# A graph layer and a routed expert layer on one core: when result rows are summed, how fast slot work is issued, batches of 6, 5 and 3, and 28 row buffers

## The chip, the cores and the metric

The kernel runs on one core of a Trainium2 chip. The metric is the device time of one execution in microseconds (us), as a median over several executions; beside it stands one profiled execution, whose trace gives the durations of single instructions. A core has five engines with their own instruction queues: PE (matmuls; PEld is its weight load), DVE (vector), ACT (scalar), POOL and SP. Each queue runs in the order in which the program issued its instructions. An instruction that waits holds up all that stand behind it on its engine. Here SP issues the plain transfers, and POOL the gathers, which fetch 128 rows by an index list.

## The reference

There are 6250 nodes of 256 features and 100,000 edges, sorted by target. First a graph layer, then a layer of 8 experts of which each node uses two:

```python
h = layernorm(x)
agg = segment_sum(h[src], dst) / maximum(degree, 1)
x = x + concatenate([h, agg], 1) @ W.T + b
t = layernorm(x)
xn = layernorm(t) * gamma + beta
w = softmax over the two largest of (xn @ Wr + br)
y = sum over those two experts e of w[e] * (gelu(xn @ W1[e] + b1[e]) @ W2[e] + b2[e])
out = x + y
```

## The kernel before

A prologue (to about 70 us) normalizes x and multiplies it by the neighbour half of W; the result goes to DRAM as `z_d`, so that the edges gather rows that are already multiplied. The own half follows as `u_d`, in pieces beside the first edges.

The edges are cut into 56 windows (`W`) of 14 tiles (`C`) of 128 edges: 784 edge tiles, counted by `t`. Per tile, POOL gathers 128 rows of `z_d` into one of `XG` buffers `xg` in a ring (`gather`, L553), and PE adds them into the window's 128 target rows by a matmul with a one-hot matrix `hot` (`add_edges`, L570), which DVE builds for seven tiles at a time (`hot_tiles`, L564). The gather issued in step `t` is that of tile `t + XG`. When a window is full, its first row is joined with the row that it shares with the window before (`shared_row` L576, by way of `keep_sums`, `put_sums`, `share_row` and SP), then divided by the degree and added to the own part (`window_x1`, L605 to L607; `load_u` fetches that part, for the last window by a POOL gather, L599), and stored as `x1_d`.

Four windows (`CW`) make a group, 14 in all. After a group's last window its nodes are normalized and routed, then sorted by expert into slots: PE sorts (L652), ACT copies runs of nodes to their slots `xe` (`copy_runs`, L786). Then comes the slot work on 128 slots for each expert: `hidden` (16 matmul instructions L811 and Gelu on ACT, L816) and `result` (8 matmul instructions L824, and DVE adds the bias and empties the single PSUM buffer `py`, L828), after which SP writes the rows to the batch's `y`. Nodes that don't fit in an expert's 128 slots go to extra tiles of the batch (`more_stages`, L854 to L879). `BATCHES` gives for each batch the number of groups and of extra tiles; a batch's rows of `y` may be gathered only when all its slot work is issued (`B.left == 0`). If the extra tiles do not suffice, a flag is set and a slow branch at the end computes everything anew.

At the end each window's result is summed: `gather_rows` loads `x1_d` through SP and gathers two rows of `y` per node on POOL (L913), `add_rows` adds them with their weights on DVE (L920, two instructions) and `store` writes the output through SP (L898), the last window through POOL (L900). That makes 112 row gathers for 56 windows.

All engines' order is written out by the program at build time. `at(t, f)` puts the routing steps of a group at fixed steps after its last window (`Steps`; `LastSteps` for the last group). `after(t)` is called after each edge tile and then on: it runs what is due, then takes slot work from the queue `tasks` as far as `pace` allows. Each piece has an assumed cost: 2.0 for half a pair of `hidden`, 1.75 for `result`, 1.7, 0.5 and 1.75 for an extra tile, so 30 for a group (8 and 8 pieces) and 3.95 for an extra tile. The pace in the edge loop is `rate`, set when a group's slot work starts (54 steps after its last window, 25 for the last group), such that each piece of work is done by its deadline; afterwards it is 2.0. `sum_rows` is called last in each step; it works with an assumed `clock`, and keeps gathers and adds apart:

```python
clock += 0.6 if t < W * C else 0.3 if tasks else 1.2
...
    spent -= us
    clock += us
```

Row sums begin when fewer than 100 tiles are left. Those that begin while edge tiles are still to be gathered use tiles of their own, `o` and `y2`; the later ones use the ring `xg` (`spare`).

Of the kernel before, what the change touches and what calls it, by code (L numbers as in the profile page):

```python
# [8 lines left out]
F32 = mybir.dt.float32  # L9
# [8 lines left out]
P = 128  # L18
EPS = 1e-5
C = 14  # L20
TB = 4
UB = 2
CW = 4
CAP = 64
BATCHES = (6, 7), (6, 5), (2, 3)
GB = 3
XG = 24


@with_exitstack  # L30
def gnn_ffn_kernel(ctx: ExitStack, tc: tile.TileContext, x, x_cols, src, dst, dst_next, gw, gw_t, gb, gb_cols, gamma, beta,
# [33 lines left out]
    N, D = x.shape  # L65
    NX, H = w1.shape[0], w1.shape[2]
# [18 lines left out]
    batches = []  # L85
    for n, tiles in BATCHES:
        B = Group()
        B.first, B.n, B.tiles = sum(b.n for b in batches), n, tiles
        B.at = HS + XS * sum(b.tiles for b in batches)
        B.more_row = n * NX * SH  # L90
        B.rows = B.more_row + XS * tiles
        B.left, B.deadline = n * NX * SH // (2 * P) + tiles, None
        batches.append(B)

    const = ctx.enter_context(tc.tile_pool(name="const", bufs=1))
# [373 lines left out]

    xg = [edges.tile([P, DA], F32, name=f"xg{i}") for i in range(XG)]  # L470
    for g in xg:
# [432 lines left out]

    def gather_rows(K, j, V):
        g = K.first + j
        gathered = now >= W * C - XG
        V.o = spare() if gathered else slots.tile([P, D], F32, name="o", bufs=2)
        nc.sync.dma_start(V.o, x1_d[g * P:(g + 1) * P, :])
        G, i = K.group, j  # L910
        V.y2 = [spare() if gathered else slots.tile([P, D], F32, name="y2", bufs=4) for _ in range(2)]
        for r in range(2):
            nc.gpsimd.indirect_dma_start(  # L913
                out=V.y2[r], out_offset=None, in_=K.batch.y[:, :],
                in_offset=bass.IndirectOffsetOnAxis(ap=G.rows[:, r, i:i + 1], axis=0))

    def add_rows(K, j, V):
        G, i = K.group, j
        for r in range(2):
            nc.vector.scalar_tensor_tensor(V.o, V.y2[r], G.w2[:, r, i:i + 1], V.o, op0=ALU.mult, op1=ALU.add)  # L920
        store(K, j, V.o)
# [1 line left out]

    tasks, later, Ks, sums, adds = [], {}, [], [], []
    slots, w1_sb, w2_sb, xe = None, None, None, None
    now, spent, rate, clock, due, spares = None, 0.0, 0.0, 0.0, 0.0, 0
    class Steps:  # L930

        x1, var, roots, norms, route, exps, weigh, choices, count = 2, 5, 7, 9, 11, 14, 15, 16, 19
# [1 line left out]
        runs, rest, place, tiles, copied, rows, pace, start = 30, 33, 36, 39, 40, 46, 1.5, 54  # L934

    class LastSteps:
# [3 lines left out]
        runs, rest, place, tiles, copied, rows, pace, start = 15, 16, 19, 24, 21, 28, 1, 25  # L940
# [37 lines left out]
        at(t + S.start, start_experts, K)  # L978

    def start_experts(K):  # L980
        nonlocal rate
        B = K.batch
        K.deadline = now + CW * C
        tasks.extend(expert_stages(K))
        if K.index == B.first + B.n - 1:
            B.deadline = now + 2 * CW * C
            tasks.extend(more_stages(B))
        Ks.append(K)
        rate, total = 0.0, 0.0
        for us, _, of in tasks:  # L990
            total += us
            rate = max(rate, 1.01 * total / max(1, of.deadline - now))
        rate = min(rate, 0.72)
        sums.extend((K, j) for j in range(CW))

    def sum_rows():

        nonlocal due
        while adds and (adds[0][0] <= clock or not (sums or tasks)):
            adds.pop(0)[1]()  # L1000
        left = W * C - 1 - now
        while sums and not sums[0][0].batch.left and clock >= due and left < 100:
            if 0 < left < XG and spares + 3 > XG - left:
                return
            K, j = sums.pop(0)
            V = Group()
            gather_rows(K, j, V)
            adds.append((clock + 8.0, lambda K=K, j=j, V=V: add_rows(K, j, V)))
            while len(adds) > XG // 3 - 1:
                adds.pop(0)[1]()  # L1010
            due = clock + 12.0 if left >= XG else max(due, clock - 6.0) + (4.0 if left > 0 else 2.4)

    def after(t):
        nonlocal now, spent, clock
        now = t
        while later.get(t):
            later[t].pop(0)()
        later.pop(t, None)
        clock += 0.6 if t < W * C else 0.3 if tasks else 1.2
        pace = rate if t < W * C else 2.0  # L1020
        spent = min(spent + pace, pace) if tasks else 0.0
        while tasks and spent > 0:
            us, f, _ = tasks.pop(0)
            spent -= us
            clock += us
            f()
        sum_rows()
# [7 lines left out]
    V = new_window(0, None)  # L1035
# [5 lines left out]
    for index in range(W // CW):  # L1041
        K = Group()
# [9 lines left out]
        for g in range(K.first, K.first + CW):  # L1052
            if g > 0:
                V = V_next
            for c in range(C):
                t = g * C + c
# [26 lines left out]
    t = W * C  # L1083
# [11 lines left out]
    with tc.If(wrong_r > 0), tc.tile_pool(name="gp", bufs=1) as gp:  # L1095
# [9 lines left out]
        with tc.For_i(0, W * C) as j:  # L1105
# [19 lines left out]
            spare = gp.tile([P, 1], F32, name="spare")  # L1125
# [110 lines left out]
```

## Time and profile before

| | |
|---|---|
| median of 3 executions | 1246.62 us (1244.07 to 1251.12) |
| profiled execution, own time | 1242.94 us |
| profiled execution, span from first to last instruction | 1240.9 us |
| busy: PE, PEld, DVE | 1039.6 (84%), 855.7 (69%), 704.7 (57%) us |
| busy: ACT, POOL | 457.3 (37%), 857.6 (69%) us |
| mean granted clock of PE | 0.944 |
| edge gathers | 784, of 0.95 us each, 70.3 to 1071.9 us |
| row gathers into `o`, `y2` | 14, 961.7 to 1060.6 us |
| row gathers into the ring | 98, 1073.1 to 1229.4 us |

A line of a group reads: source line, engine, operation, output <- inputs, count | busy time, mean ns of one | idle time of the engine just before, and what ended most of it. A line of the waits reads: engine, what waited <- for what: us in total, number of times, longest. A line of the timeline begins with start and duration in us. A busy POOL means that it writes a gather's descriptors; the rows land later (3.0 us after the start at the median of the edge gathers).

### The profile page before, as it was taken

The numbers are of one execution on the slowest core, as the hardware profiler recorded it, in microseconds if no ns is written. First come the engines' busy times: TensorE is split into PE (matmuls) and PEld (weight loads), VectorE is DVE, ScalarE is ACT, GpSimd is POOL, SyncE is SP. The second block draws the span as 40 slices with busy tenths as digits, with TensorE's granted clock in tenths as the row PEclk, the third lists the DMA queues.
The fourth block names the chain that finished last, engine by engine and source line by source line (L and its number), as shares of the span: only waits on it lengthen the run. The fifth ranks groups of instructions, "written<-read, shape, count | busy, mean of one in ns | idle before, by whom it ended". The sixth has DMA issues, their size and how long they took to land. (4 is left out here: it accounts for less than half of the span.)

```text
span 1240.9 us, 18842 instructions
## 1 busy us (share of the span) xinstructions
PE 1039.6 (84%) x5236; PEld 855.7 (69%) x5236; DVE 704.7 (57%) x2432; ACT 457.3 (37%) x1265; POOL 857.6 (69%) x907
## 2 busy tenths in 40 slices
PE   7997857699989888998989999998985787889770
PEld 6775645688867677776767988786764676758650
DVE  5765667475646465654547455564643644668442
ACT  2400002645453444353434536344342242535410
POOL 0057777777777777777777777777777777776615
PEclk9999987899999999999999999999998787999895
DMA  9989896455555545555555555555554555666644
GB/s 325 362 258 292 262 351 193 134 153 153 151 151 148 153 134 147 154 149 137 151 152 148 147 162 151 148 154 142 151 147 135 152 162 150 176 207 206 201 142 133
DMA packets 139188, 221.03 MB, mean 178 GB/s; under 512 B 23108, under 2 KB 106255, under 8 KB 138950
## 3 DMA queue, kind: packets, MB, share of 16 engines
q0 software_dynamic: 43104, 120.94, 37.4%
q1 hardware_dynamic: 87638, 89.37, 21.6%
q10 hardware_dynamic: 8336, 9.45, 2.3%
q8 instruction: 44, 0.72, 0.3%
q14 instruction: 66, 0.54, 0.1%
HBM read 166.69 MB, written 53.02 MB: 177 GB/s over the span
## 5 line engine op out<-in xcount | busy, mean ns | idle before, releaser
L553 POOL DMA_INDIRECT xg<-z_d,src_i x784 | 746.5, 952 | 307.0 <-issue 110.9
L570 PE MATMUL pS<-xg,hot 128*128 128x265 f32 x1568 | 440.2, 405 | 68.5 <-DMA xg<-z_d,src_i 50.2
L570 PEld LDWEIGHTS pS<-xg,hot 128*128 128x128 f32 x1568 | 287.3, 196 | 161.9 <-DMA xg<-z_d,src_i 86.5
L811 PE MATMUL ph<-xe,w_sb 128*128 128x128 f32 x1792 | 228.6, 283 | 21.5 <-ACT xe L786 20.7
L811 PEld LDWEIGHTS ph<-xe,w_sb 128*128 128x128 f32 x1792 | 224.9, 199 | 30.0 <-ACT xe L786 22.8
L824 PE MATMUL py<-w_sb,hid 128*128 128x256 f32 x896 | 214.9, 385 | 1.8 <-DVE rows L828 0.9
L816 ACT ACTIVATE hid<-ph,b_sb 128x128 f32<-128x128 f32 x448 | 127.4, 368 | 208.8 <-PE ph L811 208.6
L824 PEld LDWEIGHTS py<-w_sb,hid 128*128 128x128 f32 x896 | 171.0, 193 | 27.9 <-issue 2.0
L786 ACT ACTIVATE xe<-xs x448 | 139.4, 311 | 67.9 <-ACT xe L786 36.5
L564 DVE TENSOR_TENSOR hot<-cols,rel 128x896 f32<-128x896 f32 x112 | 121.1, 1081 | 72.5 <-PE pS L570 69.8
L913 POOL DMA_INDIRECT xg<-y_d,rows_i x98 | 94.7, 966 | 61.6 <-DMA y_d<-rows 25.6
L576 DVE TENSOR_TENSOR pS<-pS,row 1x265 f32<-1x265 f32 x55 | 23.5, 428 | 157.7 <-PE pS L570 146.8
L655 ACT ACTIVATE xs<-pm,beta_sb,gamma_sb 128x256 f32<-128x256 f32 x112 | 57.1, 561 | 129.3 <-PE pm L652 129.1
L580 ACT ACTIVATE sums<-pS 128x265 f32<-128x265 f32 x56 | 21.7, 388 | 178.1 <-DVE pS L576 76.5
L652 PE MATMUL pm<-to,xn 128*128 128x256 f32 x224 | 59.7, 390 | 21.6 <-DVE to L645 21.6
L255 PE MATMUL ph<-gc,x_t 128*128 128x264 f32 (+1 forms) x200 | 58.9, 420 | 15.4 <-DVE u_t L372 13.1
L920 DVE SCALAR_TENSOR_TENSOR xg<-xg,w,xg 128x256 f32<-128x256 f32 x98 | 46.5, 482 | 37.8 <-DMA xg<-y_d,rows_i 21.2
L828 DVE TENSOR_TENSOR rows<-py,b_sb 128x512 f32<-128x512 f32 x56 | 38.3, 685 | 51.9 <-PE py L824 51.7
L652 PEld LDWEIGHTS pm<-to,xn 128*128 128x128 f32 x224 | 43.2, 195 | 29.3 <-DVE to L645 21.7
L255 PEld LDWEIGHTS ph<-gc,x_t 128*128 128x128 f32 x200 | 38.7, 202 | 28.3 <-issue 13.0
L816 ACT ACT_TABLE_LOAD x24 | 30.8, 1283 | 67.4 <-PE ph L811 67.2
L255 PE MATMUL pm<-gc,x_t 128*128 128x264 f32 (+1 forms) x192 | 54.0, 406 | 0.0
(191 smaller groups left out, 840.2 us busy)
## 6 DMA issues: line engine op xcount, KB each, us to landing
y_d<-rows SPq DMA_DIRECT2D x56, 256.0 KB
xg<-z_d,src_i POOLq DMA_INDIRECT x784, 3.0
w_sb<-w_dram ACTq DMA_DIRECT2D x16, 512.0 KB
sums_d<-sums SPq DMA_DIRECT2D x55, 132.5 KB
x<-u_d SPq DMA_DIRECT2D x55, 132.0 KB
x_d<-x SPq DMA_DIRECT2D x56, 128.0 KB
u_d<-u_t SPq DMA_DIRECT2D x24, 264.0 KB
xg<-x_d SPq DMA_DIRECT2D x49, 128.0 KB
```

Source lines behind the costliest of these rows:

```text
L255: nc.tensor.matmul(pz, x_t[:, t, k, :], gc[:, h * KD + k, :n], start=(k == 0), stop=(k == KD - 1))
L553: nc.gpsimd.indirect_dma_start(out=xg[(g * C + c) % XG][:, :DZ], out_offset=None, in_=z_d[:, :], in_offset=bass.IndirectOffsetOnAxis(ap=sr ...
L564: nc.vector.tensor_tensor(hot, col[:, None, :].to_broadcast([P, HC, P]), V.rel[:, c:c + HC, None].to_broadcast([P, HC, P]), op=ALU.is_equal)
L570: nc.tensor.matmul(V.pS, V.hot[c // HC][:, c % HC, :], xg[(V.g * C + c) % XG], start=(c == 0), stop=(c == C - 1))
L652: nc.tensor.matmul(px[:, k, :], G.xn[i][:, k * P:(k + 1) * P], G.one_hot[i], start=True, stop=True)
L655: nc.scalar.activation(xs[:, at:at + 2 * P], px[:, k, :], AF.Identity, bias=beta_sb[:, k:k + 1], scale=gamma_sb[:, k:k + 1])
L786: nc.scalar.activation(xe[:, :, bass.ds(to_at, CAP)], src[:, :, bass.ds(src_at, CAP)], AF.Copy)
L811: nc.tensor.matmul(ph[:, i, a * SH:(a + 1) * SH], w1_sb[:, U.e + a, k, c * P:(c + 1) * P], xe[:, k, at:at + SH], start=(k == 0), stop=(k = ...
L816: nc.scalar.activation(U.hid[:, c, a * SH:(a + 1) * SH], ph[:, i, a * SH:(a + 1) * SH], AF.Gelu, bias=b1_sb[:, U.e + a, c:c + 1])
L824: nc.tensor.matmul(U.py[:, h, :], U.hid[:, c, h * P:(h + 1) * P], w2_sb[:, U.e + h, c, :], start=(c == 0), stop=(c == KH - 1))
L913: nc.gpsimd.indirect_dma_start(out=V.y2[r], out_offset=None, in_=K.batch.y[:, :], in_offset=bass.IndirectOffsetOnAxis(ap=G.rows[:, r, i:i ...
L920: nc.vector.scalar_tensor_tensor(V.o, V.y2[r], G.w2[:, r, i:i + 1], V.o, op0=ALU.mult, op1=ALU.add)
```

## The change

The second batch has five groups instead of six, the third three groups instead of two; the extra tiles stay at 7, 5 and 3. The ring has 28 buffers instead of 24, and so edge gathers are issued 28 tiles ahead. Row sums begin when fewer than `XG` = 28 tiles are left, which is after the last edge gather is issued, and they use the ring alone; `o` and `y2` are gone. The add of a window is put 10 instead of 8 on the assumed clock after its gathers, and eight instead of seven adds may be open. The deadlines go: the pace of slot work is 0.72 in the edge loop, 1.2 after it until the last group's slot work starts, then 2.0.

```diff
-BATCHES = (6, 7), (6, 5), (2, 3)
+BATCHES = (6, 7), (5, 5), (3, 3)
 GB = 3
-XG = 24
+XG = 28
...
     def gather_rows(K, j, V):
         g = K.first + j
-        gathered = now >= W * C - XG
-        V.o = spare() if gathered else slots.tile([P, D], F32, name="o", bufs=2)
+        V.o = spare()
         nc.sync.dma_start(V.o, x1_d[g * P:(g + 1) * P, :])
         G, i = K.group, j
-        V.y2 = [spare() if gathered else slots.tile([P, D], F32, name="y2", bufs=4) for _ in range(2)]
+        V.y2 = [spare() for _ in range(2)]
...
     def start_experts(K):
-        nonlocal rate
         B = K.batch
-        K.deadline = now + CW * C
         tasks.extend(expert_stages(K))
         if K.index == B.first + B.n - 1:
-            B.deadline = now + 2 * CW * C
             tasks.extend(more_stages(B))
         Ks.append(K)
-        rate, total = 0.0, 0.0
-        for us, _, of in tasks:
-            total += us
-            rate = max(rate, 1.01 * total / max(1, of.deadline - now))
-        rate = min(rate, 0.72)
         sums.extend((K, j) for j in range(CW))
...
         left = W * C - 1 - now
-        while sums and not sums[0][0].batch.left and clock >= due and left < 100:
+        while sums and not sums[0][0].batch.left and clock >= due and left < XG:
             if 0 < left < XG and spares + 3 > XG - left:
                 return
             K, j = sums.pop(0)
             V = Group()
             gather_rows(K, j, V)
-            adds.append((clock + 8.0, lambda K=K, j=j, V=V: add_rows(K, j, V)))
+            adds.append((clock + 10.0, lambda K=K, j=j, V=V: add_rows(K, j, V)))
             while len(adds) > XG // 3 - 1:
                 adds.pop(0)[1]()
-            due = clock + 12.0 if left >= XG else max(due, clock - 6.0) + (4.0 if left > 0 else 2.4)
+            due = max(due, clock - 6.0) + (4.0 if left > 0 else 2.4)
...
         clock += 0.6 if t < W * C else 0.3 if tasks else 1.2
-        pace = rate if t < W * C else 2.0
+        pace = 0.72 if t < W * C else 1.2 if len(Ks) < W // CW else 2.0
```

More of the change, by code (lines that the diff above doesn't have):

```diff
@@ L91, in gnn_ffn_kernel @@
         B.rows = B.more_row + XS * tiles
-        B.left, B.deadline = n * NX * SH // (2 * P) + tiles, None
+        B.left = n * NX * SH // (2 * P) + tiles
         batches.append(B)
@@ L928, in gnn_ffn_kernel @@
     slots, w1_sb, w2_sb, xe = None, None, None, None
-    now, spent, rate, clock, due, spares = None, 0.0, 0.0, 0.0, 0.0, 0
+    now, spent, clock, due, spares = None, 0.0, 0.0, 0.0, 0
     class Steps:
```

## The prediction

> **What bounds the kernel now.** The chain that ended last holds two pieces only (the final scatter), so I read the other views: the costliest groups first, then busy time in stretches of 50 us, the waits, and the timeline of the last 300 us.
>
> ```profile
> L553 POOL DMA_INDIRECT xg<-z_d,src_i x784 | 746.5, 952 | 307.0 <-issue 110.9
> L913 POOL DMA_INDIRECT xg<-y_d,rows_i x98 | 94.7, 966 | 61.6 <-DMA y_d<-rows 25.6
> ```
>
> The 784 edge gathers take 952 ns each, with 0.30 us between two. The first starts at 70.3, tile 672 at 915.3: one per 1.257 us. Counting the rows of L570 beside those of L553, PE consumes tile 196 to tile 672 only 2 to 5 us behind POOL, about what a gather needs to land (3.0 us median). So through the middle **POOL sets the pace** and PE follows. Then, by stretch (PE, PEld, DVE, ACT, POOL, clock, DMA share, GB/s):
>
> ```profile
> 650.00:700.00 50.00, 50.00 (x257) 41.19 (x256) 36.00 (x129) 23.91 (x68) 37.82 (x40) 1.00 0.55 147
> 700.00:750.00 50.00, 49.64 (x288) 43.71 (x287) 28.75 (x90) 23.38 (x63) 37.93 (x40) 1.00 0.56 155
> ...
> 950.00:1000.00 50.00, 31.96 (x148) 27.15 (x147) 22.16 (x76) 14.39 (x42) 37.81 (x41) 0.80 0.51 140
> 1000.00:1050.00 50.00, 35.73 (x183) 31.23 (x181) 24.08 (x81) 15.46 (x40) 37.81 (x41) 0.83 0.57 158
> ...
> 1200.00:1250.00 50.00, 6.61 (x33) 5.06 (x31) 9.71 (x20) 2.28 (x8) 16.27 (x17) 0.67 0.32 95
> ```
>
> From 950 to 1050 PE loses 18.0 + 14.3 = 32 us while POOL goes on. The waits name it, and a second hole:
>
> ```profile
> DVE o L920 <- DMA y<-y_d,rows_i: 48.9, 11, 21.0
> POOL xg L913 <- DMA y_d<-rows: 25.6, 1, 25.6
> ```
>
> The first: an early add of result rows stands in DVE's queue for a gather that POOL reaches only after the edge gathers issued ahead of it. DVE sits from 943.5 to 964.5:
>
> ```profile
> 943.31 0.17 DVE L640 TENSOR_SCALAR q<-q 128x8 f32<-128x8 f32 x1
> 964.48 0.48 DVE L920 SCALAR_TENSOR_TENSOR o<-y,w,o 128x256 f32<-128x256 f32 x1 [20.99 <-DMA y<-y_d,rows_i]
> ```
>
> After it PE is some 20 us behind POOL and stays there: the last edge gather starts at 1071.9, its matmul at 1092.3.
>
> ```profile
> 1071.88 0.95 POOL L553 DMA_INDIRECT xg<-z_d,src_i  x1 [0.30 <-PE pS L570]
> 1092.33 0.61 PE L570 MATMUL pS<-xg,hot 128*128 128x265 f32 x2
> ```
>
> The second hole is the end: POOL is out of rows it may gather at 1185 and waits for the last batch's y.
>
> ```profile
> 1207.43 0.43 DVE L876 TENSOR_TENSOR rows<-py,b_sb 128x256 f32<-128x256 f32 x1 [2.15 <-PE py L872]
> 1210.55 0.94 POOL L913 DMA_INDIRECT xg<-y_d,rows_i  x1 [25.57 <-DMA y_d<-rows]
> 1229.42 0.95 POOL L913 DMA_INDIRECT xg<-y_d,rows_i  x1 [0.30 <-issue]
> 1233.73 1.02 POOL L900 DMA_INDIRECT out_dram<-xg,tail_i  x1 [3.36 <-DVEq L1095]
> ```
>
> So the end is: last y evacuated (Y = 1207.9), 2.7 us until POOL gathers it, 16 gathers with 15 steps of 1.25, and 11.5 us from the start of the last gather to the end at 1240.9.
>
> **What the skill says.** "Perfetto Trace Analysis", DMA Instruction — SWDGE (GPSIMD): the profiled end of a gather is the end of descriptor writing, not of the move. The trace agrees: 0.95 us on POOL, 3.0 us to landing. The same page, What "DMA-bound" means: a kernel can be bound by the issuing engine's descriptor work; POOL's unbroken 37.8 of 50 us with the DMA engines at 0.55 is that. "TensorE: Matmul & The Clock Gate", HAM oscillation: idle gaps over about 3.4 us cost PE its clock; in the two stretches with the holes the granted clock is 0.80 and 0.83, else 1.00 around them.
>
> **The change by parts.** I count the loop by hand through its own quantities (tile t, queue of tasks, clock).
>
> *Sums behind the last edge gather.* With `left < 100` seven windows (gathers at t = 684, 695, 706 ...) put 14 row gathers among the edge gathers; with `left < 28` the first stands at t = 758, behind the last edge gather (t = 755). POOL drops 14 x 1.25 = 17.5 us ahead of the last edge gather: 1071.9 - 17.5 = 1054.4 (70.3 + 783 x 1.257 = 1054.5 agrees). The 14 gathers, 7 loads of x1 and 7 stores on SP are not removed but come later; all 112 row gathers now run after 1054, against 98.
>
> The wait on DVE is moved, not gone. Add 0 goes to t = 766. DVE arrives when tile 766 is consumed: 70.3 + 766 x 1.257 + 4 = 1037. Its second row gather starts at 1057 and lands 3.2 us later (median of L913): 1060.5. **A stall of 23 us**, like the 21.0 of before. Queued behind it on DVE: evacuations L828 (py has one buffer, so PE stops at the next result), hot tiles of window 55 (L564, t = 770), and L576, L605 to L607 of windows 54 and 55; on SP the store, then put_sums and share_row of window 54. From there add j can run at 1060.5 + 2.5 j. The last window's L605 (t = 785) stands behind add 6 (t = 784): 1075.5 + 1 = 1076.5. POOL's own queue is later still: the last window's x1 gather L599 (t = 782) stands behind 16 row gathers, 1055.7 + 16 x 1.25 = 1075.7, and lands 3.2 later, 1079; so L607 runs at 1079 where it ran at 1096.3 (L599 was behind 12 of them, at 1088.6, and not late). **17 us earlier**: what POOL saves, with the same lag as before. The stalls from 943 on go, but only this net counts.
>
> *Slot work at 0.72.* A group is 8 hidden (2.0) and 8 result (1.75), 30 us; an extra tile 3.95. The trace's durations fit: 16 matmuls of L811 in 1.95, 8 of L824 in 1.89. Before, group 11 starts at t = 725 with 30 + 19.75 for batch 1's five tiles, at rate 1.01 x 30 / 56 = 0.541; at 784 there are left 16.3 of tiles and 30 of group 12, 46.3 us, all done before group 13 starts (t = 808). After, batch 1 ends with group 10, its tiles run by t = 735, group 11 is done by 777, and group 12 has 26 us left at 784, which 1.2 a step takes in the 24 steps. **20 us less** PE work between the last window and group 13. Before, that stretch took 1096.3 to 1151.4 (first L811 of group 13), 55 us with PE at 43 of 50, so less work shortens it; 35 remain. Does DVE allow that? Adds 7 to 20 stand in it: 14 x 2.5 = 35. Just.
>
> Does 0.72 overfill PE earlier? Before ran at 0.72 too, for t = 445 to 613 (about 635 to 845 us): PE was full there, its lag at most 7 us, POOL undisturbed. Cost nothing; the cover is the ring and the 14 of 56 steps that a group then leaves free. Without it POOL would lose the 7 us once per group at most.
>
> *28 buffers.* 35 us of ring for 30. POOL never stood for a full ring in the edge stage, so no gain; four more memsets, and 4.2 KB per partition against 6 KB of o and y2 given up: nothing. Unknown cost of a changed layout: I take 0, ends -1 and +3 (the page's 0.3 us idle before a gather, some ten times). Delay 10 for 8 and eight open adds for seven give the rows more time: in with the stalls.
>
> *Batches 6, 5, 3.* 15 extra tiles as before, but after the last y there are 24 gathers, not 16: **8 x 1.25 = 10 us more at the end**.
>
> Sum on the profiled span: Y = 1207.9 - 17 - 20 = 1171; end = 1240.9 - 37 + 10 = **1214**. Check by POOL: 88 gathers from 1055.7 at 1.25 end at 1166, at before's own 1.367 (81 steps in 1073.1 to 1183.9) at 1176. The last 24 then start between 1171 + 2.7 and 1176, giving 1214 to 1216. I take 1214. The profiled execution took 1242.94, 2.0 over its span; the median 1246.62 is 3.7 above that. So 1214 + 5.7 is **1220**. Floor: 897 gathers (784, 112 and L599), 896 steps of 1.25 from 70.3 with no hole, and the same 11.5: 1202, so 1208.
>
> **Rivals.** (1) *The stall eats the rest.* The last group's routing is chained to adds that POOL paces, so only the 17.5 us reach Y: 1240.9 - 17.5 + 10 + 5.7 = 1239. For it: the 35 against 35 above. Against it: in 1075 to 1210 DVE waited only 4.0 us for row gathers. (2) *Slower: the ring of rows becomes the bound.* An add also needs the x1 load, and SP takes loads and stores in order; DVE waited 14.9 us for x1, up to 3.0 each. If each window cost 1.0 of adds and 3.0 of waiting, a gather takes 2.0 us: 1055.7 + 111 x 2.0 + 11.5 + 5.7 = 1295. It decides from 1.61 us a gather (slower by 0.5%), 1.56 for no gain; before showed 1.367 with seven open adds. (3) *It doesn't do what it says*: a fixed 0.72 leaves the last groups as they were, and only the 10 us more and the 17.5 less remain (as rival 1), or 5 or 3 extra tiles don't hold the batches' tokens and the slow branch runs; counted from the inputs they need 5 and 2, so that is out.
>
> **How the numbers follow.** A measurement of this kernel can tell about 0.5% (6.2 us) from no change. Forecast 0.75, rival 1 0.14, rival 2 0.06, rest 0.05. Rival 1 lies at the edge of faster and same: half to each. Faster 0.86, same 0.08, slower 0.06. Range: the floor less one for the layout, 1207, to rival 1 with one more, 1240.
>
> **What would show it.** Right: last L553 at about 1054; no L913 before it; a DVE wait on y_d gathers of 20 us or more at about 1037; PE over 40 of 50 us in 950 to 1000; Y near 1171; POOL's wait for y_d under 8 us; 24 gathers after it. Wrong: POOL slower than 1.26 us in the edge stage; row gathers over 1.5 us apart; Y after 1185.

## The result and the profile after

The changed kernel takes 1242.74 us at the median of 10 executions (1239.93 to 1244.05); the kernel before, run again beside it, 1246.68 (1243.91 to 1251.12). The ratio is 0.9967, with a 95% interval of 0.9953 to 0.9981: faster by a third of a per cent, where 2% were forecast. The profiled execution takes 1243.91 us, its span 1242.0. In three of the five batches of runs below every kernel, the one before among them, took 17 to 18% longer (before: 1453 to 1468 us), which is called the slower condition.

The groups of the kernel after, from its page:

```profile
L553 POOL DMA_INDIRECT xg<-z_d,src_i x784 | 747.7, 954 | 306.3 <-issue 115.5
L912 POOL DMA_INDIRECT xg<-y_d,rows_i x112 | 108.5, 969 | 61.4 <-issue 19.8
```

All 112 row gathers are now one group, and an edge gather costs what it did. The stretches (PE, PEld, DVE, ACT, POOL, clock, DMA share, GB/s):

```profile
950.00:1000.00 50.00, 50.00 (x233) 39.35 (x233) 30.77 (x106) 20.87 (x66) 37.81 (x41) 1.00 0.56 154
1000.00:1050.00 50.00, 49.75 (x294) 44.69 (x293) 31.73 (x117) 23.45 (x63) 37.81 (x41) 1.00 0.56 157
1050.00:1100.00 50.00, 31.55 (x176) 27.73 (x175) 26.38 (x84) 19.48 (x56) 36.82 (x38) 0.83 0.63 185
```

The hole of 950 to 1050 is filled: PE 50.00 and 49.75 where it had 31.96 and 35.73. A new one opens behind the last edge gather, and the granted clock falls to 0.83 there, as the Trainium skill, "TensorE: Matmul & The Clock Gate", HAM oscillation, would have it (PE stands idle for 12.3 us at one point). The timeline of the kernel after around the last edge gather, DVE's part and POOL's:

```profile
1059.43 0.48 DVE L919 SCALAR_TENSOR_TENSOR xg<-xg,w,xg 128x256 f32<-128x256 f32 x1 [12.08 <-DMA xg<-y_d,rows_i]
...
1054.90 0.95 POOL L553 DMA_INDIRECT xg<-z_d,src_i  x1 [0.30 <-issue]
1056.16 0.94 POOL L912 DMA_INDIRECT xg<-y_d,rows_i  x1 [0.30 <-issue]
```

The last edge gather starts at 1054.90, forecast 1054.4, and the first row gather directly after it. DVE stands for that row, 12.1 us instead of the forecast 23. And the end, in the same view:

```profile
1191.39 0.42 DVE L876 TENSOR_TENSOR rows<-py,b_sb 128x256 f32<-128x256 f32 x1 [2.15 <-PE py L872]
...
1196.75 0.94 POOL L912 DMA_INDIRECT xg<-y_d,rows_i  x1 [10.45 <-DVE xg L919]
1226.04 0.95 POOL L912 DMA_INDIRECT xg<-y_d,rows_i  x1 [0.30 <-issue]
1235.16 1.02 POOL L900 DMA_INDIRECT out_dram<-xg,tail_i  x1 [8.18 <-SPq L1086]
```

The last y is 16 us earlier than before, not 37. POOL needs 5.4 us instead of 3.1 from the start of that L876 to the next gather, then 24 gathers follow, and 16.0 us instead of 11.5 from the last of them to the end.

With the prediction's own steps, ends and lengths in us:

| step | forecast | measured | difference |
|---|---|---|---|
| last window's L607 | 1079 | 1083.2 | +4.2 |
| L607 to the last group's first L811 | 35 | 45.4 | +10.4 |
| from there to the last y (L876) | 57 | 62.8 | +5.8 |
| last y to the next row gather | 2.7 | 5.4 | +2.7 |
| 23 steps of gathers | 28.8 | 29.3 | +0.5 |
| last gather to the end | 11.5 | 16.0 | +4.5 |
| span | 1214 | 1242.0 | +28 |

The forecast counts y to the end of its L876, the measured column to its start, 0.4 us earlier.

### The profile page after: what moved, and what is told of

It is laid out like the page before. It is cut to its first block, busy times and chain, and to the rows that moved or that the text cites. A ratio compares the mean times of both kernels' runs of the same rounds, so it can differ in the third digit from the quotient of the medians.

```text
span 1242.0 us, 18821 instructions
## 1 busy us (share of the span) xinstructions
PE 1024.7 (83%) x5236; PEld 870.2 (70%) x5236; DVE 705.5 (57%) x2436; ACT 454.6 (37%) x1264; POOL 859.5 (69%) x907
## 5 line engine op out<-in xcount | busy, mean ns | idle before, releaser
L570 PE MATMUL pS<-xg,hot 128*128 128x265 f32 x1568 | 418.5, 398 | 20.1 <-issue 7.3
L570 PEld LDWEIGHTS pS<-xg,hot 128*128 128x128 f32 x1568 | 295.8, 196 | 78.7 <-issue 14.9
L811 PE MATMUL ph<-xe,w_sb 128*128 128x128 f32 x1792 | 237.3, 290 | 68.2 <-ACT xe L786 68.2
L811 PEld LDWEIGHTS ph<-xe,w_sb 128*128 128x128 f32 x1792 | 233.7, 205 | 79.5 <-ACT xe L786 73.1
L824 PE MATMUL py<-w_sb,hid 128*128 128x256 f32 x896 | 219.0, 390 | 13.5 <-DVE rows L828 13.5
L816 ACT ACTIVATE hid<-ph,b_sb 128x128 f32<-128x128 f32 x448 | 128.1, 369 | 243.5 <-PE ph L811 243.2
L824 PEld LDWEIGHTS py<-w_sb,hid 128*128 128x128 f32 x896 | 172.0, 195 | 42.4 <-ACT xe L786 13.0
L912 POOL DMA_INDIRECT xg<-y_d,rows_i x112 | 108.5, 969 | 61.4 <-issue 19.8
L919 DVE SCALAR_TENSOR_TENSOR xg<-xg,w,xg 128x256 f32<-128x256 f32 x112 | 52.8, 483 | 37.6 <-DMA xg<-y_d,rows_i 34.9
L255 PE MATMUL ph<-gc,x_t 128*128 128x264 f32 (+1 forms) x200 | 56.1, 404 | 11.8 <-DVE u_t L372 7.3
L652 PE MATMUL pm<-to,xn 128*128 128x256 f32 x224 | 57.6, 380 | 2.7 <-DVE to L645 2.7
L652 PEld LDWEIGHTS pm<-to,xn 128*128 128x128 f32 x224 | 42.4, 190 | 9.7 <-issue 3.0
```

The lines of the kernel that those rows point to most:

```text
L255: nc.tensor.matmul(pz, x_t[:, t, k, :], gc[:, h * KD + k, :n], start=(k == 0), stop=(k == KD - 1))
L570: nc.tensor.matmul(V.pS, V.hot[c // HC][:, c % HC, :], xg[(V.g * C + c) % XG], start=(c == 0), stop=(c == C - 1))
L652: nc.tensor.matmul(px[:, k, :], G.xn[i][:, k * P:(k + 1) * P], G.one_hot[i], start=True, stop=True)
L811: nc.tensor.matmul(ph[:, i, a * SH:(a + 1) * SH], w1_sb[:, U.e + a, k, c * P:(c + 1) * P], xe[:, k, at:at + SH], start=(k == 0), stop=(k = ...
L816: nc.scalar.activation(U.hid[:, c, a * SH:(a + 1) * SH], ph[:, i, a * SH:(a + 1) * SH], AF.Gelu, bias=b1_sb[:, U.e + a, c:c + 1])
L824: nc.tensor.matmul(U.py[:, h, :], U.hid[:, c, h * P:(h + 1) * P], w2_sb[:, U.e + h, c, :], start=(c == 0), stop=(c == KH - 1))
```

## The experiments

The question was where the forecast 37 us of the last y went, and what the last three rows are made of. The **slot-work theory** is the prediction's: what PE does in the stretch between the last window and the last group sets its length, one for one. The first **rival** is that the row sums, in DVE's and SP's queues, hold up the last group. The second is that the last group's routing has a length of its own, from hand-overs between DVE, PE and ACT, under which less slot work brings nothing.

Every ratio is to the kernel before in its own batch. The kernel before has no profile in the slower condition, and the kernel after was not run in it as it is.

### Row sums held back, left out, or stored elsewhere

All three start from the kernel after. The first lets no row sum begin before the last slot work is issued, so its time must be long and only its last group is of interest. It ran three times, twice in the slower condition:

```diff
-        while sums and not sums[0][0].batch.left and clock >= due and left < XG:
+        while sums and len(Ks) == W // CW and not tasks and clock >= due and left < XG:
```

> The changed kernel, but no row is gathered, added or stored before the last slot work is issued; all 112 row gathers come then. The span must be long (the last y + 3 + 111 x 1.25 + 16); what counts is the time from the last window's L607 to the last y's L876, 108.6 us in the changed kernel and 111.6 in the kernel before. Theory chain: 100 or more. Theory rows: 85 or less. Theory PE: the same slot work, 105 to 109.

> The changed kernel, but no row is gathered, added or stored before the last slot work is issued; all 112 row gathers come then. What counts is the time from the last window's L607 to the last y's L876, 108.2 us in the profile of the changed kernel and 111.1 in that of the kernel before. Theory rows (adds on DVE and stores on SP of the row sums stand in the path of the last group): 85 or less, most of the gain between L607 and the first copy_runs and behind the last hidden. Theory chain (the path's own hand-overs): 100 or more. Theory PE (slot work behind the last edge): 105 to 109.

> The changed kernel with all row sums held until the last slot work is issued, once more beside the changed kernel on one chip. Theory rows: L607 to the last y some 96 us if the chip is the one of the runs before, 85 or less if it is one on which the kernel before takes 1246; in the changed kernel beside it 30 or more longer. Theory chain: no more than 10 apart.

The second leaves the two adds of rows out, and the third stores the sums to `x1_d`, so that the output stays unwritten:

```diff
         for r in range(2):
-            nc.vector.scalar_tensor_tensor(V.o, V.y2[r], G.w2[:, r, i:i + 1], V.o, op0=ALU.mult, op1=ALU.add)
...
-            nc.sync.dma_start(out[window_rows(g), :], o)
+            nc.sync.dma_start(x1_d[g * P:(g + 1) * P, :], o)
```

> The changed kernel with the adds of row sums on DVE left out (112 instructions of 0.48 us; rows are gathered and the loaded x1 rows stored, so the output lacks the expert part). Theory rows by DVE: no stall on the first gathered row, L607 to the last y 20 us or more shorter than in the changed kernel beside it, the span 15 or more shorter. Theory rows by SP: L607 to y under 8 us shorter, since stores still form a chain. Theory chain and theory PE: within 4 us.

> The changed kernel with 55 of 56 output stores going to the window's own rows of x1_d instead of the output (whose rows overlap between windows, so that each store waits until the one before has landed); the output is not written. Theory rows by SP (stores in a chain of one landing each hold up the y writes, the x1 loads and the ring): L607 to the last y 10 us or more shorter than in the changed kernel beside it, the tail from the last row gather to the end 5 or more shorter, no wait of POOL on stores; the span 10 to 20 shorter. Theory rows by DVE (adds in DVE's queue): L607 to y within 3 us, the span under 6 shorter. Theory chain and theory PE: nothing but the tail.

The kernel after was run beside them as it is, and once more in the last batch:

> The changed kernel as it is, beside the experiments: on the chip that these runs have had, the kernel before takes 1453 to 1468 us and PE, with pauses of its own, and not POOL sets the pace of the edges. If the pace of 0.72 costs there what it cost alone (ratio 1.013), the changed kernel is slower than the kernel before, ratio 1.005 to 1.02; if the late sums and the batches decide, 0.99 to 1.00. From the last window's L607 to the last y 135 to 145 us with rows in between, against 96 without.

> The changed kernel as it is, for the chip that this call gets. On one where the kernel before takes 1246: ratio 0.997, L607 to the last y 108. On one where it takes 1453 to 1468, theory pace (0.72 costs there what it cost alone, 1.011 to 1.013, since PE and not POOL is short and the burst fills the ring): ratio 1.008 to 1.015, and L607 to the first hidden 62 to 64 us like that of the run with most of group 12's matmuls left out (62.7 and 63.9), since below some 33 us of slot work the routing's hand-overs decide. Theory PE: 18 us longer than without those matmuls, 80.

| kernel | median | ratio (95%) | L607 | to L811 | to y | to gather | last gather to end |
|---|---|---|---|---|---|---|---|
| after, beside them | 1244.43 | 0.9983 (0.9962 to 1.0003) | 1079.3 | 45.4 | 63.0 | 6.7 | 14.7 |
| after, last batch | 1242.41 | 0.9987 (0.9970 to 1.0004) | 1080.6 | 45.2 | 66.1 | 3.5 | 16.0 |
| stores elsewhere | 1231.20 | 0.9889 (0.9859 to 0.9918) | 1085.0 | 43.8 | 57.6 | 5.1 | 10.6 |
| no adds | 1229.95 | 0.9879 (0.9848 to 0.9909) | 1081.3 | 38.3 | 57.8 | 11.9 | 14.5 |
| sums held back | 1319.32 (one run) | | 1069.3 | 38.6 | 57.8 | | |

In the slower condition the kernel with held sums took 1537.09 and 1560.54 us (one run each), and from L607 to the last y 96.4 and 96.2 us, against 96.3 in the run of the table. None of the forecasts for it came true: 96 us lie between the 85 or less of the rows theory and the 100 or more of the chain theory. The kernels without adds and with stores elsewhere have 12.4 and 7.0 us less from L607 to y than the kernel after beside them, where 20 and 10 or more were named.

The stretches of the last group, L607 to first L811 and from there to y, tell most (columns as in the stretches above). First the kernel before:

```profile
1096.29:1151.36 55.07, 46.96 (x276) 40.09 (x273) 41.67 (x135) 29.00 (x82) 40.02 (x42) 1.00 0.70 207
1151.36:1207.43 56.07, 45.24 (x242) 37.54 (x242) 23.70 (x61) 15.94 (x56) 22.71 (x24) 0.94 0.58 176
```

The kernel after:

```profile
1083.18:1128.59 45.41, 30.21 (x165) 26.14 (x163) 36.23 (x128) 21.11 (x57) 34.56 (x36) 0.91 0.69 208
1128.59:1191.39 62.80, 50.45 (x242) 41.31 (x242) 21.72 (x54) 15.97 (x56) 32.46 (x34) 0.85 0.56 170
```

The kernel with the sums held back:

```profile
1069.32:1107.89 38.57, 28.91 (x164) 25.38 (x163) 22.30 (x96) 21.05 (x57) 8.30 (x9) 0.93 0.21 65
1107.89:1165.64 57.75, 48.90 (x242) 41.22 (x242) 7.39 (x20) 15.97 (x56) 0.00 (x0) 0.81 0.07 24
```

And the kernel without the adds:

```profile
1081.26:1119.58 38.32, 21.42 (x100) 18.13 (x100) 22.46 (x96) 17.54 (x48) 29.12 (x31) 0.79 0.75 221
1119.58:1177.39 57.81, 48.95 (x242) 41.27 (x242) 7.39 (x21) 15.96 (x56) 37.92 (x40) 0.81 0.63 190
```

Three things follow. PE has 16.8 us less to do in the first stretch of the kernel after than before (46.96 to 30.21), of which its slot work, counted by line, is 19.3 (45.7 to 26.4: the forecast 20). But the stretch is only 9.7 us shorter, and PE's idle time in it went from 8.1 to 15.2 us: the work left, and waiting took its place. Second, with the sums away the stretch takes 38 us, with 25.4 us of slot work in it (held back) as with 17.6 (no adds); what these 38 us are is told below. Third, the two stretches together take 96 us with the adds gone, whether POOL gathers all along (29.12 and 37.92 us busy) or not (8.30 and 0.00). So neither the gathers nor the memory traffic (190 to 221 GB/s against 24 to 65) slow the last group; the 12 us more of the kernel after go with the adds, 7 in the first stretch and 5 in the second.

The kernel with its stores elsewhere says how much of this is SP's. It keeps the adds, and has 43.8 and 57.6: the second stretch is back at its own length, the first is not. SP's waits from 1055 us on, in the kernel after:

```profile
SPq L898 <- DMA out_dram<-xg: 54.3, 42, 3.3
```

With the stores elsewhere no such row is left. (That edit also spares SP the reading of each store's first row number, which is known at run time only.) Each store of a sum waits in SP's queue until the one before it has landed, and SP writes `y` in the same order. A result on DVE needs one of three buffers `rows`, and a buffer comes free when its write to `y` has landed. Two rows of DVE's waits between L607 and the last y, in the kernel after:

```profile
DVE rows L858 <- DMA y_d<-rows: 4.8, 2, 4.2
DVE rows L828 <- DMA out_dram<-xg: 2.6, 1, 2.6
```

DVE stands 7.4 us for a buffer, and not at all with the stores elsewhere; the adds themselves wait 0.9 us there. So SP's stores make 7 of the 12 us (101.5 for 108.5 beside it), most of it in the second stretch, and 4 to 5 at the end. It takes the adds as well: without them the stores wait as long (55.7 us), and yet DVE does not stand for a buffer; how the two work together was not followed. The other 5 us stay while the adds stay: 32 adds of 0.48 us stand among the steps of the routing in DVE's queue in the first stretch alone. The last four stores of the kernel after are one piece of SP's timeline:

```profile
1225.65 7.21 SPq L898 DMA_DIRECT2D out_dram<-xg  x4
```

Three steps in 6.9 us, 2.3 a store. The Trainium skill, "DMA: Bandwidth & Descriptors", Anatomy of one DMA — SWDGE (gpsimd) path, puts about 2.0 us on a transfer whatever its size, most of it the wait for the write's receipt, and 128 KB at its rate adds an estimated 0.3. The section is on transfers that POOL issues; the trace shows the same sum for these, which SP issues, but not how it divides. The final scatter L900 waits 8.18 us for SP.

Leaving the adds out moved y by 10 us, to 1177.4, but POOL then waited 12.4 us for the write of y, behind SP's stores. The gain at y was turned into a new wait, and the span (1232.6) came out near that of the stores elsewhere (1231.4). Both edits in one kernel were not run.

L607 itself shows the same. With sums held back it comes at 1069.3, 14 us after the last edge gather; in the kernel after, 28 us after it. PE's last L570 comes at 1064.6 in the first and 1078.5 in the second, because DVE's wait for the first rows (12.1 us) keeps `py` full, and PE waits 12.3 us for it at L824. Without adds L570 comes at 1064.5 again, but L607 only at 1081.3, 24 us after its last edge gather: now it waits 12.0 us for its own gather L599, which stands behind 16 row gathers. The two hold-ups lie beside each other, so removing the first alone brought 4 of the 14 us at L607. The second alone was not removed.

### What the 38 us are

PE's part of the timeline with the sums held back divides them:

```profile
1081.65 0.68 PE L625 MATMUL pm<-both,ones 128*128 128x64 f32 x2 [3.63 <-DVE both L619]
...
1082.52 4.97 PE L824 MATMUL py<-w_sb,hid 128*128 128x256 f32 x16
1087.33 1.03 PE L652 MATMUL pm<-to,xn 128*128 128x256 f32 x4
1088.19 1.95 PE L811 MATMUL ph<-xe,w_sb 128*128 128x128 f32 x16
...
1097.20 1.03 PE L652 MATMUL pm<-to,xn 128*128 128x256 f32 x4
...
1107.89 1.43 PE L811 MATMUL ph<-xe,w_sb 128*128 128x128 f32 x5 [6.02 <-ACT xe L786]
```

First come normalizing and routing on DVE and ACT, up to PE's L625, which counts the group's tokens; then the sorts on PE, up to the last L652; then the copies on ACT. In us:

| kernel | L607 to L625 | to the end of the last L652 | to the first L811 |
|---|---|---|---|
| before | 24.5 | 19.1 | 11.4 |
| after | 14.9 | 20.5 | 10.0 |
| sums held back | 12.3 | 16.6 | 9.7 |
| no adds | 9.7 | 17.8 | 10.8 |

The gain of the kernel after over the one before, 9.7 us, is all in the first piece, in which the kernel before still has the extra tiles on PE. In the second piece PE has no pause with the sums held back, and what it does there is not the sorts alone: 12 to 14 us of group 12's slot work stand between them in PE's queue, in the same order in the last two kernels. The slot work by which these two differ lies outside that piece. So the 38 us are not hand-overs only, and that slot work counts for nothing below some length is not shown; no run took the work between the sorts away in the condition of the prediction.

The hand-overs behind the sorts can be read off the timeline of the kernel after, PE's part and then ACT's:

```profile
1128.59 3.78 PE L811 MATMUL ph<-xe,w_sb 128*128 128x128 f32 x16 [5.88 <-ACT xe L786]
1134.83 1.44 PE L811 MATMUL ph<-xe,w_sb 128*128 128x128 f32 x5 [2.46 <-ACT xe L786]
...
1132.41 1.14 ACT L816 ACTIVATE hid<-ph,b_sb 128x128 f32<-128x128 f32 x4 [3.87 <-PE ph L811]
1133.42 1.35 ACT L786 ACTIVATE xe<-xs  x4
```

The last group's first L811 waits 5.9 us for the copies of nodes into their slots, with nothing else left for PE; the next one waits 2.5 us, because the copies that it needs stand on ACT behind the Gelu of the one before. A step takes 6.2 us (1128.59 to 1134.83) for 3.8 us of PE. Only a kernel in the slower condition changed the copies (next part), so their share in the 38 and the 57.8 us is read from the trace, not shown by a run.

### Less slot work behind the last edge

Two more kernels start from the kernel after, in the slower condition. In the first, group 12's slot work is thinned (one of the two input halves in `hidden`, one of four parts in `result`, so its results are left incomplete); in the second, the last group's copies come faster:

```diff
-                    for k in range(KD):
+                    n = 1 if K.index == 12 else KD
+                    for k in range(n):
...
-            for c in range(KH):
+            n = 1 if K.index == 12 else KH
+            for c in range(n):
...
```

> The changed kernel with most of group 12's matmuls left out (in hidden only k = 0, in result only c = 0 are multiplied, so that group's rows are not the full sums): about 18 of its 30 us of PE work, which run between tile 781 and the start of group 13, are gone; all else is as in the changed kernel. Theory PE: the last y 15 us or more earlier, the span 1227 or less. Theory chain and theory rows: the last y moves by under 5 us, span 1237 to 1242.

> The changed kernel with most of group 12's matmuls left out (in hidden only k = 0, in result only c = 0, so that this group's rows are not the full sums): some 18 us of PE work between tile 781 and the start of group 13 are gone. On a chip where the kernel before takes 1246: theory PE (the prediction's step, slot work between the last window and group 13 is on the path): L607 to the first hidden 15 us shorter than the 45.4 of the changed kernel, ratio to the kernel before 0.985 or less. Theory chain and rows (the path is the routing's own hand-overs, 96 us, plus what the row sums put in front of it, 12): L607 to the first hidden 40 or more, ratio 0.993 or more.

```diff
-        runs, rest, place, tiles, copied, rows, pace, start = 15, 16, 19, 24, 21, 28, 1, 25
+        runs, rest, place, tiles, copied, rows, pace, start = 15, 16, 19, 24, 21, 22, 0.5, 25
```

> The changed kernel with two of the last group's steps earlier: find_rows (PE L756, DVE L760) at step 22 instead of 28, so ahead of the group's hidden, and copy_runs two a step, so that all eight are issued ahead of the first hidden. DVE waited 15.9 us at L760 for L756, which stood behind three hidden; each of the first hidden waited for the copy before it, which stood behind the Gelu of the hidden before. Theory chain: the last hidden of the ping-pong 6 us earlier, the last y 5 to 8 earlier, span 1234 to 1237. Theory rows: the adds that stood behind L760 run 15 us earlier and free DVE and SP later, so the last y 8 to 12 earlier, span 1230 to 1234. Theory PE: no change in PE work, span 1240 to 1242.

The thinned kernel took 1485.78 and 1488.74 us, ratios 1.0123 (1.0077 to 1.0168) and 1.0105 (1.0053 to 1.0157). Its first stretch, in the second run:

```profile
1291.60:1355.51 63.91, 20.99 (x75) 16.48 (x74) 35.91 (x128) 20.90 (x57) 31.86 (x33) 0.61 0.48 142
```

The same stretch of a kernel of the same batch with the whole slot work (the kernel after with a quiet last window, described last):

```profile
1290.12:1353.27 63.15, 36.68 (x165) 29.79 (x163) 39.77 (x137) 21.06 (x57) 35.03 (x36) 0.78 0.56 165
```

15.7 us less PE work, and the stretch is no shorter. This says less than it seems. The two kernels differ in the place of their adds too, and in both ACT stands about 16 to 18 us in this stretch (L816, L817 in the thinned kernel) for something that the trace doesn't show. With the sums held back the stretch took 38.5 us in this condition as well, both times, so some 25 of these 63 us come with the sums; under them slot work was not the bound. The other edit moved the copies earlier on the clock and took 1487.44 us, 1.0149 (1.0087 to 1.0211), with 74.6 us from L607 to L811; no gain is to be seen, and why was not pursued.

### One part at a time

Three kernels take the change apart: before with the later start of row sums alone (three runs), before with the pace of the kernel after alone (two), and after with the batches of before:

```diff
-        while sums and not sums[0][0].batch.left and clock >= due and left < 100:
+        while sums and not sums[0][0].batch.left and clock >= due and left < XG:
...
-        pace = rate if t < W * C else 2.0
+        pace = 0.72 if t < W * C else 1.2 if len(Ks) < W // CW else 2.0
...
-BATCHES = (6, 7), (5, 5), (3, 3)
+BATCHES = (6, 7), (6, 5), (2, 3)
```

> The kernel before with one edit: row sums start behind the last edge gather (left < XG = 24). Theory PE (the slot work left behind the last edge is on the path to the last y, as the prediction had it): the last edge gather at 1054, the last window's L607 some 13 us earlier (1083), nothing else changed, so the last y 13 earlier (1195) and the span about 1228. Theory rows (adds on DVE and stores on SP of the row sums stand in the path of the last group): seven more windows of sums now lie in that stretch, so L607 gains 13 but the last y gains under 7: span 1234 or more. Theory chain (the last group's path is a chain of hand-overs between DVE, PE and ACT with its own length): as theory PE here, 1228.

> The kernel before with one edit: row sums start behind the last edge gather (left < XG = 24). Theory PE and theory chain: the last window's L607 13 us earlier (1083), nothing else changed, so the last y 13 earlier (1195), span about 1228. Theory rows: seven more windows of sums lie between L607 and the last y; the last y gains under 5 us, span 1236 or more, and L607 to y takes 116 or more.

> The kernel before with the late sums alone. On a chip where the kernel before takes 1246: the last edge gather at 1055, L607 13 us earlier. Theory PE: L607 to the last y 111 as before, the last y 13 earlier, ratio 0.99. Theory rows: L607 to y 115 or more because seven more windows of rows fall into it, ratio 0.993 to 1.0.

> The kernel before with one edit: the pace of the slot work is 0.72 in the edge loop, 1.2 behind it until the last group starts, then 2.0. Behind tile 784 some 33 us of slot work are left instead of 46. Theory PE: the last y 13 us earlier, span about 1228. Theory chain and theory rows: slot work is off the path, the last y moves by under 4 us, span 1237 to 1242.

> The kernel before with the pace of slot work alone (0.72, 1.2, 2.0). On a chip where the kernel before takes 1246: theory PE: 13 us less slot work behind the last edge, L607 to the last y 98, ratio 0.99 or less. Theory chain and rows: L607 to y 106 or more, ratio 0.995 to 1.003.

> The changed kernel with batches of 6, 6 and 2 groups again. Behind the last y there are 16 gathers instead of 24, 10 us less; behind tile 784 about 7 us more slot work (extra tiles of batch 1). Theory PE: the last y 7 us later, span 3 us shorter, 1239. Theory chain: the last y where it was (1192), span 10 shorter, 1232. Theory rows: the ready windows are the same ones, more of them, all summed before the last y: 8 more gathers, adds and stores in front of it, so the last y 5 or more later and the span about 1237.

| kernel | median | ratio (95%) | last edge gather | L607 to y |
|---|---|---|---|---|
| late sums | 1451.19 | 0.9984 (0.9968 to 1.0000) | 1217.6 | 159.5 |
| late sums, again | 1466.35 | 0.9988 (0.9974 to 1.0002) | 1228.6 | 164.4 |
| late sums, again | 1465.58 | 0.9992 (0.9979 to 1.0006) | 1231.7 | 158.6 |
| pace | 1472.19 | 1.0130 (1.0086 to 1.0175) | 1251.3 | 140.9 |
| pace, again | 1486.17 | 1.0112 (1.0074 to 1.0151) | 1264.9 | 141.2 |
| after, batches of before | 1466.78 | 1.0079 (1.0060 to 1.0099) | 1236.3 | 140.7 |

The pace alone costs 1.1 to 1.3% in this condition. What it does is best seen between the late sums and the kernel after with the batches of before, of one batch of runs, which both have late sums: with the pace (and the 28 buffers and longer delay) the last group's stretches are 18.8 us shorter (140.7 for 159.5), but the last edge gather comes 18.7 us later (1236.3 for 1217.6). The kernel with the pace alone still has 14 row gathers ahead of its last edge gather, so not all of its 33 us there are the pace's. The late sums alone bring 0.1 to 0.2%, at the edge of what can be told. All three parts of the change were tried in the slower condition only; what each is worth alone in the condition of the prediction stays open.

### A quiet last window

The last kernels take the two hold-ups of L607 away together. The last window's L599 is issued at tile 763, ahead of the row gathers, and no add is put before the last window's L607; then one a step while slot work is left:

```diff
-        while adds and (adds[0][0] <= clock or not (sums or tasks)):
-            adds.pop(0)[1]()
         left = W * C - 1 - now
+        while left < -1 and adds and (adds[0][0] <= clock or not (sums or tasks)):
+            adds.pop(0)[1]()
+            if tasks:
+                break
...
+            if left > -2 and len(adds) == XG // 3 - 1:
+                return
...
                     V_next = new_window(g + 1, V)
+                    if g + 1 == W - 1:
+                        load_u(V_next)
...
-                if c == HC + 5:
+                if c == HC + 5 and g < W - 1:
```

This was done once in the kernel after, in the slower condition, and once in the kernel before with late sums, 28 buffers, the ring alone and the delay of 10, that is with the deadlines and the batches 6, 6, 2 kept:

> The changed kernel with the row sums kept out of the way of the last window: its x1 gather (L599) is issued at tile 763 instead of 782, so behind 2 windows of row gathers and not 8; no add stands in DVE's queue before the last window's L607, and then one a step while there is slot work. On a chip where the kernel before takes 1246, theory rows: L607 at 1070 instead of 1083 (as with rows held, 1069), L607 to the last y 96 to 106, the last y at 1168 to 1177 instead of 1191, the next gather no sooner than POOL is through with the 88 ready ones (1166 to 1180); span 1218 to 1228, ratio 0.978 to 0.99. Theory chain alone: L607 the same 13 earlier, but then POOL and the stores decide: ratio 0.99 or more.

> The kernel before (its deadlines' pace, its batches of 6, 6, 2) with the late sums, 28 buffers, the last window's x1 gather at tile 763, no add in DVE's queue before the last window's L607, and then one a step while there is slot work. Theory rows (sums in front of the last window and the last group cost the time; slot work behind the last edge costs less than its 46 us): on a chip where the kernel before takes 1246, L607 at 1070 instead of 1096, L607 to the last y 105 to 115, 16 gathers behind it, span 1215 to 1230, ratio 0.975 to 0.988. On a chip where PE sets the pace of the edges (before 1453 to 1468), L607 to y 150 to 160 as with late sums alone, but L607 earlier by 5: ratio 0.990 to 0.998. Theory PE (46 us of slot work stand in the path): the gain of L607 is lost between L607 and y, ratio 0.993 or more on either chip.

The first took 1483.27 us, 1.0101 (1.0068 to 1.0134), and what the edit alone did there can't be told without a run of the kernel after in that condition. The second took **1226.70 us, a ratio of 0.9863 (0.9839 to 0.9886)**: it beats both kernels. Its timeline at L607, the last y, and the first and last gather of the end:

```profile
1063.14 0.49 DVE L607 SCALAR_TENSOR_TENSOR x<-pS,rdeg,x 128x264 f32<-128x264 f32 x1 [0.97 <-DMA x<-u_d,tail_i]
...
1187.41 0.42 DVE L876 TENSOR_TENSOR rows<-py,b_sb 128x256 f32<-128x256 f32 x1 [1.24 <-PE py L872]
...
1194.37 0.94 POOL L912 DMA_INDIRECT xg<-y_d,rows_i  x1 [15.74 <-DMA xg<-x_d]
...
1213.34 0.95 POOL L912 DMA_INDIRECT xg<-y_d,rows_i  x1 [0.30 <-issue]
```

L607 is 20 us earlier than in the kernel after: 1.8 by the last edge gather (1053.1), 4 because PE is some 3 us behind POOL with the deadlines and some 10 with 0.72 (last L570 5.2 us after the last edge gather, 9.3 with 0.72 and sums held back), the other 14 by the wait of DVE and L599. Of these 20 us, 16 go again on the way to y (124.3 us against 108.2), where the deadlines leave 19 us more slot work (45.4 to 26.4, by line) and the adds now wait, 16.3 us for x1 and 13.6 for rows of y; the runs don't part the two. So y comes only 4 us earlier, and most of the 17.6 us of span are in the end: 16 gathers instead of 24, 10.3 us, and 11.1 instead of 16.0 us behind the last. y to gather takes 1.6 more. The mean granted clock is 0.959, after 0.924, before 0.944.

## Why the prediction missed

**Right**: POOL drops 14 gathers ahead of the last edge gather (1054.9 for 1054.4), the first hole goes (PE 49.75 and more of 50), the 28 buffers cost nothing that shows, eight more gathers stand behind the last y (24 for 16, 10.4 us for 10), and there is 19.3 us less slot work for 20. The sign was right.

**The step that failed** is "so less work shortens it; 35 remain". PE at 43 of 50 was read as the bound of the stretch. It was only the most used engine of it: 19.3 us of work left, 9.7 us came off, and 45.4 remained. Of the 10.4 us that are missing, 3.5 would have been missing with no sums at all (38.3 to 38.6), and the larger part, 7, came with the adds. The question "Does DVE allow that? ... Just." was the right one, but 35 against 35 counted the time in which gathers bring the rows, as if DVE had nothing else to do. It was busy for 36.2 of the 45.4 us, and a step of the routing stands behind every add that was put ahead of it, whether that add waits or not. That the 3.5 us are a chain through DVE, PE and ACT is read from the trace.

**The stretch to y** was taken as 57 unchanged, and came to 62.8: its own 57.8, as forecast, and 5 us that go when SP's stores go; DVE stands there for buffers whose writes to `y` are behind those stores. **The end** was taken at 2.7 and 11.5 as before, and came to 5.4 and 16.0. The 16.0 are the store chain (10.6 without it), which the prediction didn't price. The 5.4 are not: with the stores elsewhere they are 5.1, and the kernel after had 3.5 to 6.7 in its other profiles. POOL's wait ends there with an add that frees a buffer of the ring; no run changed that alone. The waits of the kernel before, from 1055 us on, had the store chain in SP's queue, of which the prediction shows no waits:

```profile
SPq L898 <- DMA out_dram<-xg: 47.0, 36, 3.2
```

More sums packed behind the last edge gather means more of them in that chain at the end. Rival 2 named SP's order, but by the load of x1, and priced it on the gathers: the 88 gathers before the last y ran from 1056.16 to 1185.36, 1.48 us each, under its point of 1.56.

**The wait on DVE** was 12.1 us for 23, because PE and DVE ran 10 us or more behind POOL rather than 4. That lag goes with the pace of 0.72, costed at nothing: the one profile outside the slower condition that has late sums and the deadlines, the last kernel above, shows 3 to 5 us, but differs in the batches too. It had no cost in POOL's gathers, as forecast, but by the trace it comes back at L607, 1083.2 for 1079. In the slower condition the pace alone cost 1.1 to 1.3%.

**Rival 1** (1239) came nearest, with the last y at 1190 for 1191.4, in part by luck: L607 gained 13 us, not 17.5, the first stretch gained 9.7 us where the rival has nothing, and the second lost 6.7. Its mechanism, adds that hold the last group's routing, is the one that the runs show, with 12 us; but SP's stores and DVE's own time make them, not POOL.

**Size**: 28 us in the span. The median is 0.7 us over the span where 5.7 were assumed, so the miss is 22.7 us there; those 5 us were luck. One reading was wrong without weight: the granted clock was 1.00 ahead of the two stretches with holes, but 0.90 in the 50 us after them.

## What to carry to other kernels

An engine that is busy most of a stretch is not yet its bound: before work is taken off it, follow the stretch from its end back through every engine's order, and let the gain end where that chain no longer holds the work. Work put into an engine's queue ahead of the chain costs its own time, even when it never waits. When work is packed behind an event, read the waits of every queue that it uses, the one that only issues transfers too; stores that wait for one another cost a fixed time each. Two hold-ups of one instruction that lie beside each other should go together: here the first alone brought 4 of 14 us.

## What the runs showed of the hardware

Stores from SP to the output, each waiting for the one before, came 2.3 us apart for 128 KB. In the slower condition a POOL gather costs the same (950 to 953 ns, for 950 to 956), but the engines show pauses that have no releaser in the trace, such as these rows of PE and ACT in the kernel before with late sums:

```profile
PE ph L811 <- issue: 76.0, 81, 2.6
ACT hid L816 <- remote: 121.3, 16, 21.1
```

In the other condition PE's rows of the first kind come to 2.5 us in the kernel before, and no kernel has a row of the second; in the slower one DVE and POOL have such rows too. One chip showed both conditions, in two batches of runs. The last group with the sums held back took the same 96 us in both, while with sums it took 133 to 164 us in the slower condition and 101 to 124 in the other. What makes the pauses is not visible in the trace and stays open.
